# Expert results added into the residual stream in DRAM by accumulating scatters, in place of a gather by token at the end

## The chip, the cores and the metric

The kernel runs on one core of one Trainium2 chip. The time of a run is the device time of that core in microseconds (us). Three runs of the kernel before took 2021.2, 2023.53 and 2025.5 us; the median is 2023.53 us. A further execution was taken with the hardware profiler; its own time is 2023.36 us, and the span of its records, from the first to the last instruction, is 2021.5 us. Instants below are microseconds from the start of that span.

The engines are TensorE (PE: matrix products and transposes; PEld is its weight load), VectorE (DVE), ScalarE (ACT), GpSimd (POOL) and SyncE (SP). SP and ACT issue ordinary DMAs, and POOL issues the indirect ones, whose row numbers come from a tile of integers. Each engine takes its instructions in order, and waits at each for the semaphores that it names.

## What is computed

One decoder layer over 4 sequences of 1024 tokens, 256 wide, all in float32, in three blocks. The first is a gated delta rule with convolutions, the second a cross-attention over 77 context rows; each is followed by a layer norm. The third is a mixture of 8 experts, of which every token uses two:

```python
router_logits = xf @ router_w.T
probs = softmax(router_logits)
topv, topi = top_k(probs, 2)
probs = probs * mask                      # the two largest are kept
probs = probs / (probs.sum(-1) + 1e-9)
h = silu(xf @ gate_w[e] + gate_b[e]) * (xf @ up_w[e] + up_b[e])
expert_out[e] = h @ down_w[e] + down_b[e]
y = einsum('ne,ned->nd', probs, expert_out)
x = layernorm(x + y)
```

(The lines from `h` on stand for every expert `e`; the reference computes all eight and multiplies six by zero.) The result is the last `x`, 4 x 1024 x 256.

## The kernel before

The tokens are worked in 8 slabs. Slab `i` has 128 tokens of each of the 4 sequences, so a tile of 128 partitions x 4 x 256. The delta rule writes its layer-normed output to `xd`, a DRAM tensor with a row for each token. The cross-attention stage reads slabs back from `xd` into SBUF tiles `xs` (three buffers, `slab_in`), adds the attention's result and norms in place. It runs over 64 units (slab, sequence, half of the heads); the steps of one unit are interleaved with those of the next ones and with the routing of the slab finished last.

`route(i)` finds for each token of slab `i` its two experts. `sel[:, 0]` and `sel[:, 1]` are one-hot rows for the first and the second expert, `share` their two normed weights, `slots` the two row numbers at which the token's vector goes into `xg`, a DRAM tensor with a region of rows for each expert. POOL then scatters the slab's rows into `xg` (L1134): 8 indirect DMAs for each slab, 128 rows of 1 KB each. Slabs 0 to 4 are written back to `xd` (L1142) so that their buffers can take slabs 3 to 7; slabs 5 to 7 stay in SBUF.

Then the weights of all experts lie in SBUF (`wall`, `wdn`, and the biases `ball`), and a list of 71 tiles (NT) is made by `tiles()`: each tile is 128 consecutive rows of one expert in `xg`. `ei` and `ri` have the expert and the first row of each tile, as integers that engines load into registers. The rows behind the last token of an expert are zeros (L1258). Tiles that no expert needs point at a region of zeros.

The tile loop (L1330) runs five steps in a staggered order: in pass `j`, `fetch(j+3)`, `hidden(j)`, `turn_h(j-1)`, `turned(j+1)`, `down(j-2)`. `fetch` is a DMA of SP from `xg` into a tile `mx`. `turned` transposes it on PE, and ACT copies it out. `hidden` multiplies by the gate and up weights (L1292, 8 matmuls), adds the gate bias on DVE (`sge`, L1300), takes silu on ACT (L1301), adds the up bias on DVE (`pup`, L1302) and multiplies on DVE (`mh`, L1304). `turn_h` transposes that, `down` multiplies by the down weights (`pdn`, L1319), DVE adds the bias into `my` (L1327, three buffers), and SP writes `my` to row `j*128` on of `yg`, a DRAM tensor of tile results (L1328).

At the end `combine(i)` works slab after slab. For each of the 4 sequences and both experts POOL gathers 128 rows from `yg` by the token's row numbers `found` (L1345), DVE multiplies them by `share` and adds them to the slab (L1351). Then come the statistics of the layer norm on DVE (L1355, L1356), its root on ACT (L1359), two small operations on DVE (L1360, L1361), the normalisation on ACT (L1363, one activation for each sequence), and one DMA to the output (L1366).

The order of instructions on each engine is set when the kernel is built: a scheduler takes, on every engine, work of later steps ahead of work that it expects to be ready later. It also places the semaphore waits: a write to a tile's buffer waits until every reader of the tile that had the buffer before it is done, and for a DMA that is its landing.

Of the kernel before, what the change touches and what calls it, by code (L numbers as in the profile page):

```python
# [17 lines left out]
P = 128  # L18
# [25 lines left out]
NROW = NE * STRIDE + NE * P  # L44

EW = 2 * KC * FF
EV = FC * D
# [18 lines left out]
N_LT = N_ROWS + 2 * H * 4  # L66
N_FREE = N_LT + NE * NE
N_STEP = N_FREE + NE
# [4 lines left out]
def _consts():  # L73
    k = np.arange(P)[:, None]
    c = np.arange(P)[None, :]

    sq = np.zeros((NSQ, P, P), np.float32)
    sq[K_ID] = k == c
    sq[K_LE] = k <= c
    sq[K_GT] = k > c  # L80
    sq[K_NGE] = -1.0 * (c >= k)
    sq[K_ONE] = 1.0
    narrow = np.zeros((P, NNARROW), np.float32)
    narrow[:, N_POS : N_POS + SC] = np.arange(SC)
# [19 lines left out]
def kernel(ctx: ExitStack, tc: tile.TileContext, a: dict, out: bass.AP):  # L104
# [14 lines left out]
    def new_banks(name, bufs):  # L119
# [20 lines left out]

    xg = tc.dram_tile([NROW, D], F32, name="xg")
    yg = tc.dram_tile([NT * P, D], F32, name="yg")

# [5 lines left out]
    nc.sync.dma_start(out=bd, in_=br)  # L149
    zero = const.tile([P, 1, D], F32, name="zero")  # L150
    nc.gpsimd.memset(zero, 0.0)

    nc.scalar.dma_start(
        out=xg[NE * STRIDE :, :].rearrange("(p r) d -> p r d", p=P), in_=bc(zero, [P, NE, D])
    )
# [3 lines left out]

    xd = tc.dram_tile([NS * B * P, D], F32, name="xd")  # L160

# [628 lines left out]
    def slab_in(pool, i):  # L790
        xs = pool.tile([P, B, D], F32, tag="xs", name="xs", bufs=3)
        nc.sync.dma_start(out=xs, in_=tokens(i))
        return xs
# [140 lines left out]
    def queries(n):  # L934

        t = units[n]
        if t["half"] == 0:
            x = slabs[t["i"]][:, t["b"], :]
# [69 lines left out]
    def outputs(n):  # L1008
# [28 lines left out]
        if half == 1:  # L1037
            x = slabs[i][:, b, :]
            nc.vector.tensor_tensor(x, x, px[:, 0:D], ALU.add)
            layernorm(xp, x, x, "c")  # L1040

    slots, found = (ek.tile([P, NS, B, 2], I32, name=n) for n in ("slots", "found"))
    at = ek.tile([P, NS, B, 2], F32, name="at")
    share = ek.tile([P, NS, B, 2], F32, name="share")

# [6 lines left out]
    def route(i):  # L1052
# [60 lines left out]
        nc.vector.tensor_tensor(got, pair, bc(pw.unsqueeze(2), [P, B, 2, NE]), ALU.mult)  # L1113
        nc.vector.tensor_reduce(share[:, i], got, AX.X, ALU.add)
        nc.vector.tensor_reduce(red, share[:, i], AX.X, ALU.add)
        nc.vector.tensor_scalar_add(red, red, 1e-9)
        nc.vector.reciprocal(red, red)
        nc.vector.tensor_tensor(share[:, i], share[:, i], bc(red.unsqueeze(2), [P, B, 2]), ALU.mult)
        yield
# [8 lines left out]
        nc.vector.tensor_tensor(got, pair, bc(place.unsqueeze(2), [P, B, 2, NE]), ALU.mult)  # L1128
        nc.vector.tensor_reduce(at[:, i], got, AX.X, ALU.add)
        nc.vector.tensor_copy(slots[:, i], at[:, i])  # L1130
        for b in range(B):
            yield
            for k in range(2):
# [5 lines left out]
                )  # L1139
                apart(ins, "scatter")  # L1140
        if i + 3 < NS:
            nc.sync.dma_start(out=tokens(i), in_=xs)  # L1142
            slabs.append(slab_in(sp, i + 3))
# [52 lines left out]
    def tiles():  # L1196


        def t(name, shape, dt=F32):
# [21 lines left out]
        )  # L1221
        ex_, row = t("tex", [P, NT]), t("trow", [P, NT])
        nc.vector.tensor_reduce(ex_, past, AX.X, ALU.add)
# [9 lines left out]
        nc.vector.tensor_copy(ri, row)  # L1233

        n = NS * B * 2
        flat = at.rearrange("p i b k -> p (i b k)")
        gap = t("gap", [P, n, NE])
        behind = nw[:, N_FREE : N_FREE + NE]
        nc.vector.tensor_scalar(nt, nt, 1.0 * P, -1.0 * STRIDE, ALU.mult, ALU.add)
        nc.vector.scalar_tensor_tensor(  # L1240
            gap, bc(flat.unsqueeze(2), [P, n, NE]), -1.0 * STRIDE, bc(behind.unsqueeze(1), [P, n, NE]), ALU.add, ALU.is_gt
        )
        nc.vector.tensor_tensor(gap, gap, bc(nt.unsqueeze(1), [P, n, NE]), ALU.mult)
        moved = t("moved", [P, n])
        nc.vector.tensor_reduce(moved, gap, AX.X, ALU.add)
        nc.vector.tensor_tensor(flat, flat, moved, ALU.add)
        nc.vector.tensor_copy(found, at)
        return ei, ri

# [3 lines left out]
    for e in range(NE):  # L1253
# [4 lines left out]
        apart(nc.sync.dma_start(out=xg[bass.ds(row, P), :], in_=zero[:, 0, :]), "scatter")  # L1258
    ei, ri = tiles()
    r_scope.close()  # L1260
# [5 lines left out]
    def fetch(j):  # L1266
# [4 lines left out]
        )  # L1271
        t["x"] = ep.tile([P, D], F32, tag="mx", name="mx", bufs=4)
        nc.sync.dma_start(out=t["x"], in_=xg[bass.ds(t["row"], P), :])
# [40 lines left out]
    def down(j):  # L1314
# [3 lines left out]
        for f in range(FC):  # L1318
# [5 lines left out]
                stop=f == FC - 1,  # L1324
            )
        y = ep.tile([P, D], F32, tag="my", name="my", bufs=3)
        nc.vector.tensor_tensor(y, px[:, 0:D], ball[:, bass.ds(e * D + B_D, D)], ALU.add)  # L1327
        nc.sync.dma_start(out=yg[j * P : (j + 1) * P, :], in_=y)  # L1328

# [8 lines left out]
    def combine(i):  # L1338
        xs = slab_in(ep, i) if i + 3 < NS else slabs[i]
        mv = ep.tile([P, B, 2], F32, tag="mv", name="mv")  # L1340
        for b in range(B):
            x = xs[:, b, :]
            for k in range(2):
                g = ep.tile([P, D], F32, tag="part", name="part", bufs=8)
                nc.gpsimd.indirect_dma_start(  # L1345
                    out=g,
                    out_offset=None,
                    in_=yg,
                    in_offset=bass.IndirectOffsetOnAxis(ap=found[:, i, b, k : k + 1], axis=0),
                )  # L1350
                nc.vector.scalar_tensor_tensor(  # L1351
                    x, g, share[:, i, b, k : k + 1], x, ALU.mult, ALU.add
                )
            st = ep.tile([P, 6], F32, tag="st", name="st", bufs=4)
# [84 lines left out]
```

## Time and profile before

| | |
|---|---|
| median of three runs | 2023.53 us |
| the profiled execution, its own time | 2023.36 us |
| the profiled execution, its span | 2021.5 us |
| busy in the span | PE 1639.5, PEld 1166.7, DVE 1134.5, ACT 917.4, POOL 550.4 us |
| delta rule and preparation of attention | 0 to about 1000 |
| cross-attention and routing | about 1000 to 1478 |
| last loads of weights, first tiles | 1478 to 1530 |
| tile loop (from the first `my` to the last) | 1526.7 to 1926.4 |
| `combine` | 1926.4 to 2021.5 |
| gathers from `yg` in `combine` | 64, first at 1929.62, last at 2009.1 |

A "busy" time is that in which the engine executed; waiting, register work and the issue of DMAs by SP are not counted. The table of stages is read from the instants at which the groups of instructions begin and end. A DMA has two times in the profile: that of the issuing instruction, and the time from issue to landing, which is when the semaphore that tells of its end is set.

### The profile page before, as it was taken

The numbers are of one execution on the slowest core, as the hardware profiler recorded it, in microseconds if no ns is written. First come the engines' busy times: TensorE is split into PE (matmuls) and PEld (weight loads), VectorE is DVE, ScalarE is ACT, GpSimd is POOL, SyncE is SP. The second block draws the span as 40 slices with busy tenths as digits, with TensorE's granted clock in tenths as the row PEclk, the third lists the DMA queues.
The fourth block names the chain that finished last, engine by engine and source line by source line (L and its number), as shares of the span: only waits on it lengthen the run. The fifth ranks groups of instructions, "written<-read, shape, count | busy, mean of one in ns | idle before, by whom it ended". The sixth has DMA issues, their size and how long they took to land.

```text
span 2021.5 us, 28024 instructions
## 1 busy us (share of the span) xinstructions
PE 1639.5 (81%) x9524; PEld 1166.7 (58%) x9524; DVE 1134.5 (56%) x3199; ACT 917.4 (45%) x2161; POOL 550.4 (27%) x503
## 2 busy tenths in 40 slices
PE   4678888888898989969898889888839999999910
PEld 2356565657575757736676666666626666666600
DVE  4738575757585857344665656656534444444444
ACT  3435554546363645522766666666502222222212
POOL 2212222222212122141444555455510000000065
PEclk9879898989898989889999999999869999999955
DMA  3011111101010101030300110000062111111144
GB/s 111 17 32 22 32 22 31 24 22 32 17 34 20 30 16 46 16 105 20 147 22 32 41 34 32 22 32 21 22 242 73 47 46 46 45 48 45 35 141 137
DMA packets 118347, 98.97 MB, mean 49 GB/s; under 512 B 57803, under 2 KB 106303, under 8 KB 117951
## 3 DMA queue, kind: packets, MB, share of 16 engines
q1 hardware_dynamic: 108863, 77.24, 12.9%
q0 software_dynamic: 6144, 16.79, 2.6%
q10 hardware_dynamic: 3200, 3.16, 0.4%
q8 instruction: 78, 1.28, 0.3%
q14 instruction: 62, 0.51, 0.1%
HBM read 62.12 MB, written 35.03 MB: 48 GB/s over the span
## 4 chain that ended last, share of the span: by engine, by line
PE 51%; DVE 19%; ACT 11%; POOL 8%; issue 6%; DMA 5%; SPq 1%; POOLq 0%; ACTq 0%; DVEq 0%
PE pgt L1292 6%; PE pdn L1319 6%; PE pup L1292 6%; ACT sc L1001 4%; PE pp L257 3%; PE pxo L1029 3%; PE psc L984 2%; DMA part<-yg,found 2%; DVE v L269 2%; DVE kq L269 2%; PE pe L432 2%; POOL xg L1134 2%; PE pss L365 2%; DVE bp L455 2%; PE pq L949 2%
## 5 line engine op out<-in xcount | busy, mean ns | idle before, releaser
L1001 ACT ACTIVATE sc<-sc,ntop,rq 128x77 f32<-128x77 f32 x512 | 182.3, 445 | 56.3 <-DVE ntop L999 47.3
L1345 POOL DMA_INDIRECT part<-yg,found x64 | 61.2, 957 | 454.8 <-issue 442.6
L1029 PE MATMUL pxo<-vo,aT 128*128 128x256 f32 (+1 forms) x640 | 161.9, 392 | 0.0
L1301 ACT ACTIVATE sge<-sge 128x512 f32<-128x512 f32 x71 | 44.7, 630 | 253.6 <-DVE sge L1300 253.6
L257 PE MATMUL pp<-nT,wqkv 128*128 128x262 f32 x512 | 144.1, 415 | 0.0
L1292 PE MATMUL pgt<-wall,mxT 128*128 x284 | 135.6, 600 | 2.0 <-ACT mxT L1281 1.2
L1319 PE MATMUL pdn<-wdn,mhT 128*128 x568 | 134.2, 379 | 0.0
L1292 PE MATMUL pup<-wall,mxT 128*128 x284 | 133.9, 594 | 0.0
L1006 POOL TENSOR_TENSOR sc<-sc,den 128x616 f32<-128x616 f32 x64 | 77.9, 1217 | 182.8 <-DVE ntop L999 87.9
L984 PE MATMUL psc<-kbd,qT 128*128 128x154 f32 x512 | 88.7, 320 | 46.9 <-ACT qT L976 45.8
L1029 PEld LDWEIGHTS pxo<-vo,aT 128*128 128x128 f32 (+1 forms) x640 | 118.7, 196 | 13.8 <-ACT aT L1020 1.9
L949 PE MATMUL pq<-xwq,xT 128*128 128x512 f32 x256 | 121.7, 597 | 0.5 <-ACT xT L943 0.5
L984 PEld LDWEIGHTS psc<-kbd,qT 128*128 128x128 f32 x512 | 79.8, 207 | 68.4 <-ACT qT L976 51.5
L963 POOL TENSOR_TENSOR rq<-rq,nhalf 128x8 f32<-128x8 f32 x64 | 105.3, 1646 | 42.2 <-DVE rq L962 40.6
L269 DVE SCALAR_TENSOR_TENSOR kq<-pp,cols,kq 128x256 f32<-128x256 f32 x192 | 90.5, 478 | 46.3 <-ACT kq L267 44.3
L269 DVE SCALAR_TENSOR_TENSOR v<-pp,cols,v 128x256 f32<-128x256 f32 x192 | 91.3, 476 | 43.8 <-ACT v L267 42.0
L257 PEld LDWEIGHTS pp<-nT,wqkv 128*128 128x128 f32 x512 | 96.4, 201 | 32.8 <-issue 18.0
L1300 DVE TENSOR_TENSOR sge<-pgt,ball 128x512 f32<-128x512 f32 x71 | 49.1, 692 | 112.9 <-PE pgt L1292 112.9
L1319 PEld LDWEIGHTS pdn<-wdn,mhT 128*128 128x128 f32 x568 | 102.5, 190 | 11.0
L685 POOL TENSOR_TENSOR so<-so,nhalf 128x4 f32<-128x4 f32 x32 | 32.3, 1010 | 269.0 <-DVE so L684 269.0
L1020 ACT COPY aT<-pat 128x512 f32<-128x512 f32 (+1 forms) x128 | 54.7, 429 | 108.1 <-PE pat L1018 108.0
L1004 DVE TENSOR_REDUCE den<-sc 128x8 f32<-128x616 f32 x64 | 50.5, 789 | 80.7 <-ACT sc L1001 80.7
(285 smaller groups left out, 3693.1 us busy)
## 6 DMA issues: line engine op xcount, KB each, us to landing
mx<-xg SPq DMA_DIRECT2D x71, 128.0 KB, 2.0
yg<-my SPq DMA_DIRECT2D x71, 128.0 KB, 1.7
xs<-xd SPq DMA_DIRECT2D x13, 512.0 KB, 4.0
xi<-in_x SPq DMA_DIRECT2D x8, 512.0 KB, 4.1
am<-ab SPq DMA_DIRECT2D x16, 256.0 KB, 4.0
xd<-kd SPq DMA_DIRECT2D x32, 128.0 KB, 2.3
wall<-in_L_ffn_gate_w SPq DMA_DIRECT2D x8, 512.0 KB, 10.4
wall<-in_L_ffn_up_w SPq DMA_DIRECT2D x8, 512.0 KB, 10.8
```

The costliest lines, as they stand in the source:

```text
L257: mm(pp[:, 0 : 2 * (HALO + P)], lhsT=wqkv[:, kc, c * P : (c + 1) * P], rhs=nT[:, kc, 2 * j : 2 * j + 2, :].rearrange("p b t -> p (b t)"), ...
L269: nc.vector.scalar_tensor_tensor(ch, pre[:, :, n : n + P], cols[:, w0 + n : w0 + n + 1], ch, ALU.mult, ALU.add)
L949: mm(pq, lhsT=t["xT"][:, kc, :], rhs=xwq[:, kc, c0 : c0 + HH * XD], start=kc == 0, stop=kc == KC - 1,)
L963: nc.gpsimd.tensor_tensor(rq, rq, nhalf[:, :HH], ALU.pow)
L984: mm(ps[:, c * 2 * SC : (c + 1) * 2 * SC], lhsT=qT[:, 2 * g + c, :], rhs=kbd[:, half * XC // 2 + 2 * g + c, b, :], start=True, stop=True,)
L1001: nc.scalar.activation(sc[:, h], sc[:, h], AF.Exp, scale=rq[:, h : h + 1], bias=ntop[:, h : h + 1])
L1006: nc.gpsimd.tensor_tensor(sc, sc, bc(den.unsqueeze(2), [P, HH, SC]), ALU.mult)
L1020: nc.scalar.copy(aT[:w, c0:c1, :].rearrange("p c t -> p (c t)"), pt[:w, 0 : (c1 - c0) * P])
L1029: mm(px[:, 0:D], lhsT=aT[:w, c, :], rhs=vo[:w, b, half * NV + c, :], start=half == 0 and c == 0, stop=half == 1 and c == NV - 1,)
L1292: mm(ps, lhsT=t["xT"][:, c, :], rhs=wall[:, bass.ds(e * EW + off + c * FF, FF)], start=c == 0, stop=c == KC - 1,)
L1319: mm(px[:, 0:D], lhsT=t["hT"][:, f, :], rhs=wdn[:, bass.ds(e * EV + f * D, D)], start=f == 0, stop=f == FC - 1,)
L1345: nc.gpsimd.indirect_dma_start(out=g, out_offset=None, in_=yg, in_offset=bass.IndirectOffsetOnAxis(ap=found[:, i, b, k : k + 1], axis=0),)
```

## The change

Tile results are no longer stored in `yg` and gathered at the end. `xd` holds the residual stream of all 8 slabs, and each tile adds its rows to it by an indirect DMA that adds in DRAM (`compute_op=ALU.add`).

For that a tile has to know, for each of its rows, which token it is and what its share is. The rows of `xg` get 4 more numbers (`DX = D + 4`): the token's row in `xd`, the number of its first expert, and its two shares. `route` writes them into 4 more columns of the slab, so that the same scatter carries them. The zero rows carry the number of a spare row of `xd` instead (128 spare rows were added), one for each partition, and shares of zero. In `down`, DVE picks the share by comparing the first expert's number with the tile's (`mw`, three operations on one column), casts the row number to an integer (`mrow`), ACT multiplies `my` by the share, and POOL scatters. All slabs are now written to `xd`, also the last three. `tiles()` loses the calculation of `found`. `combine` loads the slab from `xd` and only norms it; its slab buffers are 4. The tile's `mx` gets 6 buffers in place of 4.

```diff
+DX = D + 4
-    xg = tc.dram_tile([NROW, D], F32, name="xg")
-    yg = tc.dram_tile([NT * P, D], F32, name="yg")
+    xg = tc.dram_tile([NROW, DX], F32, name="xg")
...
-    xd = tc.dram_tile([NS * B * P, D], F32, name="xd")
+    xd = tc.dram_tile([NS * B * P + P, D], F32, name="xd")
+    nc.scalar.dma_start(out=xd[NS * B * P :, :], in_=zero[:, 0, 0:D])
...
     def slab_in(pool, i):
-        xs = pool.tile([P, B, D], F32, tag="xs", name="xs", bufs=3)
-        nc.sync.dma_start(out=xs, in_=tokens(i))
+        xs = pool.tile([P, B, DX], F32, tag="xs", name="xs", bufs=3)
+        nc.sync.dma_start(out=xs[:, :, 0:D], in_=tokens(i))
         return xs
...
-        nc.vector.tensor_tensor(share[:, i], share[:, i], bc(red.unsqueeze(2), [P, B, 2]), ALU.mult)
+        nc.vector.tensor_tensor(xs[:, :, D + 2 :], share, bc(red.unsqueeze(2), [P, B, 2]), ALU.mult)
+        nc.vector.tensor_scalar(
+            xs[:, :, D], nw[:, N_STEP : N_STEP + B], nw[:, N_PART : N_PART + 1], float(i * B * P), ALU.add, ALU.add
+        )
+        first = rp.tile([P, B, NE], F32, tag="first", name="first")
+        number = nw[:, N_NUM : N_NUM + NE].unsqueeze(1)
+        nc.vector.tensor_tensor(first, sel[:, 0], bc(number, [P, B, NE]), ALU.mult)
+        nc.vector.tensor_reduce(xs[:, :, D + 1], first, AX.X, ALU.add)
...
+        nc.sync.dma_start(out=tokens(i), in_=xs[:, :, 0:D])
         if i + 3 < NS:
-            nc.sync.dma_start(out=tokens(i), in_=xs)
             slabs.append(slab_in(sp, i + 3))
...
-        t["x"] = ep.tile([P, D], F32, tag="mx", name="mx", bufs=4)
+        t["x"] = ep.tile([P, DX], F32, tag="mx", name="mx", bufs=6)
         nc.sync.dma_start(out=t["x"], in_=xg[bass.ds(t["row"], P), :])
...
+        e0, w = t["x"][:, D + 1 : D + 2], ep.tile([P, 2], F32, tag="mw", name="mw", bufs=4)
+        mine = ex_[:, j : j + 1]
+        nc.vector.scalar_tensor_tensor(
+            w[:, 0:1], e0, mine, t["x"][:, D + 2 : D + 3], ALU.is_equal, ALU.mult
+        )
+        nc.vector.scalar_tensor_tensor(
+            w[:, 1:2], e0, mine, t["x"][:, D + 3 : D + 4], ALU.not_equal, ALU.mult
+        )
+        nc.vector.tensor_tensor(w[:, 0:1], w[:, 0:1], w[:, 1:2], ALU.add)
+        row = ep.tile([P, 1], I32, tag="mrow", name="mrow", bufs=4)
+        nc.vector.tensor_copy(row, t["x"][:, D : D + 1])
         y = ep.tile([P, D], F32, tag="my", name="my", bufs=3)
         nc.vector.tensor_tensor(y, px[:, 0:D], ball[:, bass.ds(e * D + B_D, D)], ALU.add)
-        nc.sync.dma_start(out=yg[j * P : (j + 1) * P, :], in_=y)
+        nc.scalar.activation(y, y, AF.Identity, scale=w[:, 0:1])
+        nc.gpsimd.indirect_dma_start(
+            out=xd,
+            out_offset=bass.IndirectOffsetOnAxis(ap=row, axis=0),
+            in_=y,
+            in_offset=None,
+            compute_op=ALU.add,
+        )
...
     def combine(i):
-        xs = slab_in(ep, i) if i + 3 < NS else slabs[i]
+        xs = ep.tile([P, B, D], F32, tag="xs", name="xs", bufs=4)
+        nc.sync.dma_start(out=xs, in_=tokens(i))
         mv = ep.tile([P, B, 2], F32, tag="mv", name="mv")
         for b in range(B):
             x = xs[:, b, :]
-            for k in range(2):
-                g = ep.tile([P, D], F32, tag="part", name="part", bufs=8)
-                nc.gpsimd.indirect_dma_start(
-                    out=g,
-                    out_offset=None,
-                    in_=yg,
-                    in_offset=bass.IndirectOffsetOnAxis(ap=found[:, i, b, k : k + 1], axis=0),
-                )
-                nc.vector.scalar_tensor_tensor(
-                    x, g, share[:, i, b, k : k + 1], x, ALU.mult, ALU.add
-                )
```

More of the change, by code (lines that the diff above doesn't have):

```diff
@@ L66 @@
 N_LT = N_ROWS + 2 * H * 4
-N_FREE = N_LT + NE * NE
+N_NUM = N_LT + NE * NE
+N_FREE = N_NUM + NE
 N_STEP = N_FREE + NE
@@ L93, in _consts @@
     narrow[:, N_LT : N_LT + NE * NE] = (e[None, :] < e[:, None]).reshape(-1)
+    narrow[:, N_NUM : N_NUM + NE] = e
     narrow[:, N_FREE : N_FREE + NE] = e * STRIDE - 1
@@ L149 @@
     nc.sync.dma_start(out=bd, in_=br)
-    zero = const.tile([P, 1, D], F32, name="zero")
+    zero = const.tile([P, 1, DX], F32, name="zero")
     nc.gpsimd.memset(zero, 0.0)
+    nc.vector.tensor_scalar_add(zero[:, 0, D : D + 1], nw[:, N_PART : N_PART + 1], float(NS * B * P))
     nc.scalar.dma_start(
-        out=xg[NE * STRIDE :, :].rearrange("(p r) d -> p r d", p=P), in_=bc(zero, [P, NE, D])
+        out=xg[NE * STRIDE :, :].rearrange("(r p) d -> p r d", p=P), in_=bc(zero, [P, NE, DX])
     )
@@ L937, in queries @@
         if t["half"] == 0:
-            x = slabs[t["i"]][:, t["b"], :]
+            x = slabs[t["i"]][:, t["b"], 0:D]
             pt = bank("pxt", "pt")
@@ L1037, in outputs @@
         if half == 1:
-            x = slabs[i][:, b, :]
+            x = slabs[i][:, b, 0:D]
             nc.vector.tensor_tensor(x, x, px[:, 0:D], ALU.add)
             layernorm(xp, x, x, "c")
-    slots, found = (ek.tile([P, NS, B, 2], I32, name=n) for n in ("slots", "found"))
-    at = ek.tile([P, NS, B, 2], F32, name="at")
-    share = ek.tile([P, NS, B, 2], F32, name="share")
+    slots = ek.tile([P, NS, B, 2], I32, name="slots")
     free = ek.tile([P, NE], F32, name="free")
@@ L1113, in route @@
         nc.vector.tensor_tensor(got, pair, bc(pw.unsqueeze(2), [P, B, 2, NE]), ALU.mult)
-        nc.vector.tensor_reduce(share[:, i], got, AX.X, ALU.add)
-        nc.vector.tensor_reduce(red, share[:, i], AX.X, ALU.add)
+        share = rp.tile([P, B, 2], F32, tag="share", name="share")
+        nc.vector.tensor_reduce(share, got, AX.X, ALU.add)
+        nc.vector.tensor_reduce(red, share, AX.X, ALU.add)
         nc.vector.tensor_scalar_add(red, red, 1e-9)
         nc.vector.reciprocal(red, red)
-        nc.vector.tensor_tensor(share[:, i], share[:, i], bc(red.unsqueeze(2), [P, B, 2]), ALU.mult)
+        nc.vector.tensor_tensor(xs[:, :, D + 2 :], share, bc(red.unsqueeze(2), [P, B, 2]), ALU.mult)
[6 more added lines that the diff above has]
+        nc.vector.tensor_reduce(xs[:, :, D + 1], first, AX.X, ALU.add)
         yield
@@ L1128, in route @@
         nc.vector.tensor_tensor(got, pair, bc(place.unsqueeze(2), [P, B, 2, NE]), ALU.mult)
-        nc.vector.tensor_reduce(at[:, i], got, AX.X, ALU.add)
-        nc.vector.tensor_copy(slots[:, i], at[:, i])
+        at = rp.tile([P, B, 2], F32, tag="at", name="at")
+        nc.vector.tensor_reduce(at, got, AX.X, ALU.add)
+        nc.vector.tensor_copy(slots[:, i], at)
         for b in range(B):
@@ L1221, in tiles @@
         )
-        ex_, row = t("tex", [P, NT]), t("trow", [P, NT])
+        ex_, row = ek.tile([P, NT], F32, name="tex"), t("trow", [P, NT])
         nc.vector.tensor_reduce(ex_, past, AX.X, ALU.add)
@@ L1233, in tiles @@
         nc.vector.tensor_copy(ri, row)
[L1235 to L1239, printed above, removed]
-        nc.vector.scalar_tensor_tensor(
-            gap, bc(flat.unsqueeze(2), [P, n, NE]), -1.0 * STRIDE, bc(behind.unsqueeze(1), [P, n, NE]), ALU.add, ALU.is_gt
-        )
[L1243 to L1248, printed above, removed]
+        return ei, ri, ex_
     behind = ek.tile([P, NE], I32, name="behind")
@@ L1258 @@
         apart(nc.sync.dma_start(out=xg[bass.ds(row, P), :], in_=zero[:, 0, :]), "scatter")
-    ei, ri = tiles()
+    ei, ri, ex_ = tiles()
     r_scope.close()
@@ L1342, in combine @@
             x = xs[:, b, :]
-            for k in range(2):
-                g = ep.tile([P, D], F32, tag="part", name="part", bufs=8)
-                nc.gpsimd.indirect_dma_start(
-                    out=g,
-                    out_offset=None,
-                    in_=yg,
-                    in_offset=bass.IndirectOffsetOnAxis(ap=found[:, i, b, k : k + 1], axis=0),
-                )
-                nc.vector.scalar_tensor_tensor(
-                    x, g, share[:, i, b, k : k + 1], x, ALU.mult, ALU.add
-                )
             st = ep.tile([P, 6], F32, tag="st", name="st", bufs=4)
```

## The prediction

> **What bounds the kernel now.** I read the stages first, as the busy time of each engine in a stretch (columns: stretch and length; PE, PEld, DVE, ACT and POOL busy with counts; granted clock; DMA share; GB/s).
>
> ```profile
> 1530.00:1926.00 396.00, 395.91 (x1507) 249.60 (x1505) 170.28 (x273) 102.26 (x204) 0.00 (x0) 1.00 0.16 48
> 1926.00:2022.00 96.00, 0.00 (x0) 0.00 (x0) 44.73 (x145) 18.97 (x40) 61.22 (x64) 0.52 0.47 144
> ```
>
> The tile loop is bound by PE, 395.91 of 396 us at clock 1.00, with POOL empty. The end stage has no PE work at all: 64 gathers on POOL. Second, the DVE timeline of one tile of the loop, and of the end:
>
> ```profile
> 1840.83 0.42 DVE L1327 TENSOR_TENSOR my<-pdn,ball 128x256 f32<-128x256 f32 x1 [0.89 <-PE pdn L1319]
> 1842.55 0.69 DVE L1300 TENSOR_TENSOR sge<-pgt,ball 128x512 f32<-128x512 f32 x1 [1.29 <-PE pgt L1292]
> 1844.26 0.70 DVE L1302 TENSOR_TENSOR pup<-pup,ball 128x512 f32<-128x512 f32 x1 [1.02 <-PE pup L1292]
> 1845.07 0.69 DVE L1304 TENSOR_TENSOR mh<-pup,sge 128x512 f32<-128x512 f32 x1
> ...
> 1846.65 0.42 DVE L1327 TENSOR_TENSOR my<-pdn,ball 128x256 f32<-128x256 f32 x1 [0.89 <-PE pdn L1319]
> ```
>
> ```profile
> 1929.62 0.99 POOL L1345 DMA_INDIRECT part<-yg,found  x1 [435.61 <-issue]
> 1930.91 0.96 POOL L1345 DMA_INDIRECT part<-yg,found  x1 [0.30 <-issue]
> 1932.17 0.95 POOL L1345 DMA_INDIRECT part<-yg,found  x1 [0.30 <-issue]
> 1932.43 0.48 DVE L1351 SCALAR_TENSOR_TENSOR xs<-part,share,xs 128x256 f32<-128x256 f32 x1 [6.06 <-DMA part<-yg,found]
> ```
>
> A tile takes 5.82 us (1846.65 - 1840.83), and DVE waits for PE before three of its four operations: it has slack. At the end a gather starts every 1.25 us, and its data are there 2.81 us after its start. Third, the DMA view (median us from issue to landing):
>
> ```profile
> mx<-xg SPq DMA_DIRECT2D x71, 128.0 KB, 2.0
> xs<-xd SPq DMA_DIRECT2D x13, 512.0 KB, 4.0
> out<-xs SPq DMA_DIRECT2D x8, 512.0 KB, 3.5
> xd<-xs SPq DMA_DIRECT2D x5, 512.0 KB, 2.9
> xg<-xs,slots POOLq DMA_INDIRECT x64, 2.4
> part<-yg,found POOLq DMA_INDIRECT x64, 2.8
> ```
>
> **What goes: the gathers.** From the end of the last `my` (1925.95 + 0.42 = 1926.4) to the end of the span is 95.1 us. The new end, counted from the landing of the last scatter, with SP's queue as built (loads 0 to 3, outputs 0 and 1, load 4, outputs 2 and 3, loads 5 and 6, output 4, load 7, outputs 5 to 7; a load from the fifth on waits for the output four before it to land): load 0 lands at 4.0. A slab's statistics on DVE are (12.4 + 5.4)/8 = 2.2 us by the rows of L1355 and L1356, and the list takes two slabs before the first root, so 8.4. Root 0.30, reciprocal, L1361 and hops 1.0, four activations 2.07 (L1363 in the end stage), so output 0 issues at 11.7. Outputs 1 to 3 follow ACT and the next two slabs' statistics to 18.4; load 4 goes at 15.3 (output 0 landed, 3.5) and lands at 19.3; 2.2 + 1.0 + 2.07 later output 4 issues, and load 7 stands behind it: 25.1. It lands at 29.1, its slab is normed at 34.4, output 7 lands at 38. With 1 us to close: 39 us.
>
> **What is added beside other work.** For each tile three one-column operations on DVE (0.15 each by L171, 128x1) after `my`, inside the 1.29 us in which it waits for `pgt`; one ACT activation (0.59, as L1363), where ACT stands idle 3.59 us before L1301; one POOL instruction (about 0.95) on an empty POOL. SP loses 71 stores of 0.32 us; it had room. Fetches keep ahead, since the six `mx` buffers are freed when DVE and PE have read them, four tiles early. Without slack in the loop these would cost 71 x 0.5 on DVE; the next part says when they don't.
>
> **What is added on a path: a loop through the scatter.** In the changed kernel's instruction lists, the scheduler has moved `mw` and `mrow` of a tile up to where its `mx` has landed, four tiles early. DVE's queue per tile reads: `my` of tile s, `mw` of tile s+4, `sge`, `mrow` of tile s+4, `pup`, `mh`, `my` of tile s+1. `mrow` has 4 buffers, so `mrow` of s+4 waits for the scatter of tile s to land. That scatter was only just fed by the `my` a few instructions ahead. Behind `mrow` in DVE's queue stand `pup`, `mh` and the next `my`; PE waits for `mh`, ACT and POOL for `my`. So there is a loop: landing, hop 0.03, `mrow` 0.15, `pup` 0.80 to the start of `mh` (1844.26 to 1845.07), `mh` 0.70, `my` 0.42, hop 0.10, ACT 0.59, hop 0.30 (cast of `slots` ended 1483.20, POOL began 1483.49), and the scatter itself. Without it 3.09 us, say 3.07 since small operations overlap the next. With A the time from an accumulating scatter's start on POOL to its landing, a tile takes the larger of 5.82 and A + 3.07. The cover is gone above A = 2.75, and every microsecond more costs 67 (tiles 4 to 70 have such a wait).
>
> **A is the unknown.** Nothing in this trace adds in DRAM. From below: the plain scatter of as many rows, 2.4; an accumulating one does all of its work. Then the loop hides. From above: a gather and a scatter one after the other, 2.8 + 2.4 = 5.2; with the rows' descriptors written once (0.96 of POOL), 4.24. Rows follow each other, so reads and writes overlap in part; the middle of 2.4 and 5.2 is 3.8. I take 3.9: nearer to 4.24 than to the gather, since reading and writing DRAM are both in it.
>
> The Trainium skill, "DMA: Bandwidth & Descriptors", section "Anatomy of one DMA — SWDGE (gpsimd) path", fits a DMA as 2.0 us plus bytes over 436 GB/s; for 128 KB read twice that is an estimate of 2.6 us, the loop would hide, and the forecast would be 1977 us. The trace's gather alone is already above it, at 2.8. A rule there speaks against the change: "Rules for kernel authors" says to wait for the earlier DMA's semaphore wherever an accumulating DMA meets another access of the same bytes; the kernel does so, and by that rule alone (0.3 + A for each tile) the stage would bind only from A = 5.5.
>
> **The sum**, by the profiled execution. `my` of tile 67 begins at 1916.46; its scatter at +1.41 = 1917.87. The loop adds 67 x (3.9 + 3.07 - 5.82) = 77.1. The last four scatters land one after the other, their tiles being ready: 4 x 3.9 + 3 x 0.3 = 16.5. The end, 39. Two smaller things: before the first tile, loads run until 1501 and one more slab of 512 KB stands in that queue (2.9 us alone, DMA share 0.60 over the stretch): +2. In routing, three more DVE operations, 0.5 to 0.6 us (0.17 to 0.19 each by the rows of L1118 and L1082) for each of 8 slabs ahead of scatters that POOL's queue waits for: 0 to 5, taken as +2. Counted at nothing: rows of 1040 bytes in place of 1024 (before, SP waits 188 us for scatters in that stage in any case); the stores of slabs 5 and 6, which lie beside attention; the 6 operations that `tiles()` loses, 2.7 us on DVE before 1490.7, as the first tile waits for loads until 1501; and at the start the zeros for `xg`, which now wait for the constants to land and stand in ACT's queue ahead of three weight loads: the first needed of these was issued at 7.57, landed 5.7 later, and is first read at 22.40, so 9 us cover it. Total 1917.9 + 77.1 + 16.5 + 39 + 4 = 2054.5 of span, and 1.9 around it (2023.36 - 2021.5): 2056.4, to be held against 2023.36, which is 0.2 below the median of the runs. I say 2056. Each microsecond of A is worth 71 (67 + 4); the zero crossing is A = 3.43.
>
> **Rivals.**
> - *The addition is nearly free* (A up to 3.38): the end's gain stays. For it: the gather, which reads DRAM too, takes only 2.8. Against: it writes no DRAM. At A = 2.8 the time is 2056.4 - 1.1 x 71 = 1978; at 2.4, with the loop hidden, the last landing is 1926.4 + 0.99 + 2.4 = 1929.8, and the time 1929.8 + 39 + 4 + 1.9 = 1975. It decides below A = 3.43. Chance 0.28.
> - *It cancels*: A of 3.4 to 3.5, within 0.2% (4 us, what a measurement here can tell from no change). Chance 0.06.
> - *Rows of one DMA engine are added one behind the other.* 128 rows over 16 engines are 8 each; if each adds 0.4 us (the distance of gather and scatter, 2.8 - 2.4) to the first one's 2.8, A is 5.6, and the time 2177. For it: a packet that needs two reads. Against: plain transfers run their rows together. Chance 0.12.
> - *My forecast*: A of 3.5 to 5.2, the loop through the scatter takes PE's place, 2028 to 2149. Chance 0.54.
>
> **How the numbers follow.** Slower is 0.54 + 0.12 = 0.66, same 0.06, faster 0.28. The likeliest case's own range is 2028 to 2149; both signs hold much, so the range reaches over the cheap case, to its bound at A = 2.4 to 2.8, and up to A = 5.2: 1976 to 2149. About 0.04 lies below and 0.12 above.
>
> **What would show it.** Right: the new indirect DMA lands 3.5 to 5 us after its start; `my` to `my` is A + 3.1, near 7.0; DVE's idle time before `mrow` is released by the DMA into `xd`; PE falls from 395.91 of 396 to about 0.83 of the loop; no gathers, and about 39 us from the last landing to the end. Wrong: tiles still 5.82 apart with DVE waiting for PE, which means a small A; or an `mrow` that doesn't wait; or an end stage far from 39.

## The result and the profile after

The changed kernel takes 2042.4 us (median of seven runs, 2032.9 to 2047.1) against 2021.4 us for the kernel before in the same comparison (seven runs, 2018.9 to 2025.5). The ratio is 1.010, with a 95% interval of 1.0079 to 1.0121: the change costs 1%. The profiled execution of the changed kernel took 2041.6 us, its span is 2039.8 us; that of before is 2021.5.

The difference of the two spans, 18.3 us, has three parts, read from the first and the last `my` (1540.5 and 1990.8; before 1526.7 and 1926.0):

| | before | after | difference |
|---|---|---|---|
| start to the first `my` | 1526.7 | 1540.5 | +13.8 |
| first `my` to the last | 399.3 | 450.3 | +51.1 |
| last `my` to the end | 95.6 | 49.0 | -46.6 |

The stages of the changed kernel, in the columns of the first view of the prediction:

```profile
1530.00:1926.00 396.00, 365.78 (x1326) 214.58 (x1325) 180.35 (x474) 113.06 (x239) 90.28 (x59) 1.00 0.26 40
```

PE had been busy for 395.91 of these 396 us; now it has gaps, and 1326 matmuls fit in place of 1507 (the first 10 us of this stretch now lie ahead of the first `my`). One tile of the loop, from the timeline of DVE, ACT and POOL (start, duration, engine, line, operation; in brackets the idle time before it and what ended that):

```profile
1840.12 1.55 POOL L1340 DMA_INDIRECT xd<-my,mrow  x1 [5.01 <-ACT my L1339]
...
1843.89 0.15 DVE L1336 CAST mrow<-mx 128x1 int32<-128x1 f32 x1 [2.81 <-DMA xd<-my,mrow]
1844.02 0.70 DVE L1301 TENSOR_TENSOR pup<-pup,ball 128x512 f32<-128x512 f32 x1
1844.83 0.69 DVE L1303 TENSOR_TENSOR mh<-pup,sge 128x512 f32<-128x512 f32 x1
1845.43 0.41 DVE L1338 TENSOR_TENSOR my<-pdn,ball 128x256 f32<-128x256 f32 x1
...
1845.88 0.51 ACT L1339 ACTIVATE my<-my,mw 128x256 f32<-128x256 f32 x1 [3.33 <-DVE my L1338]
...
1846.67 1.55 POOL L1340 DMA_INDIRECT xd<-my,mrow  x1 [4.99 <-ACT my L1339]
```

This is a closed loop of 6.55 us (1846.67 - 1840.12). A scatter starts on POOL; 3.77 us later its landing lets DVE cast `mrow`, a column of 128 numbers for a tile four further on; behind that wait stand `pup`, `mh` and `my` of the next tile, and then ACT and POOL. `pup`, `mh` and `my` no longer wait for PE at all: where before each showed an idle time released by PE, or followed such a one, now they follow `mrow`. The group of `mrow` (from the costliest groups of the page: count, busy time, mean ns of one, idle time before them and what ended it) shows it for all tiles. In the chain of work that ended last (its shares of the span, by engine and line) the scatter into `xd` has the largest share:

```profile
L1336 DVE CAST mrow<-mx 128x1 int32<-128x1 f32 x71 | 10.9, 153 | 191.9 <-DMA xd<-my,mrow 191.9
```

```profile
DMA xd<-my,mrow 12%; DVE pup L1301 2%; ACT my L1339 2%; DVE my L1338 1%; DVE mh L1303 1%; DMA xs<-xd 1%; ACT xs L1371 0%; DVE st L1363 0%; DVE mrow L1336 0%; DVEq L1338 0%; DMA out<-xs 0%; DVEq L1303 0%; DVEq L1328 0%; DVE mv L1364 0%; DVE r L1368 0%
```

An operation of 0.15 us, done 71 times, has 191.9 us of waiting before it in all, and all of that is for the scatters. The DMA view (count, median us from issue to landing) has a first sign of what adding in DRAM costs: 3.8 us against 2.6 for the plain scatters into `xg` in the same kernel:

```profile
xd<-my,mrow POOLq DMA_INDIRECT x71, 3.8
...
xg<-xs,slots POOLq DMA_INDIRECT x64, 2.6
```

The end, from the timeline of POOL and SP: the last tiles' results are ready, and their scatters wait for one another; the loads of the slabs start when the last has landed.

```profile
1989.62 1.55 POOL L1340 DMA_INDIRECT xd<-my,mrow  x1 [2.98 <-DMA xd<-my,mrow]
...
1994.07 1.55 POOL L1340 DMA_INDIRECT xd<-my,mrow  x1 [2.90 <-DMA xd<-my,mrow]
...
1998.51 1.55 POOL L1340 DMA_INDIRECT xd<-my,mrow  x1 [2.89 <-DMA xd<-my,mrow]
...
2002.23 2.04 SPq L1358 DMA_DIRECT2D xs<-xd  x4
```

From 2002.23 to the end of the span are 37.5 us.

So the end is 46.6 us shorter without the gathers, as meant, the tile loop is 51.1 us longer, and 13.8 us come from a place ahead of the tiles. Two questions were put to the chip: is it this loop, and what in it; and where do the 13.8 us come from?

### The profile page after: what moved, and what is told of

Its sections match the earlier page's. It is cut to its first block, busy times and chain, and to the rows that moved or that the text cites. A ratio compares the mean times of both kernels' runs of the same rounds, so it can differ in the third digit from the quotient of the medians.

```text
span 2039.8 us, 28261 instructions
## 1 busy us (share of the span) xinstructions
PE 1674.2 (82%) x9524; PEld 1173.0 (58%) x9524; DVE 1144.2 (56%) x3438; ACT 945.2 (46%) x2232; POOL 598.7 (29%) x510
## 3 DMA queue, kind: packets, MB, share of 16 engines
q0 software_dynamic: 13296, 17.83, 5.3%
## 5 line engine op out<-in xcount | busy, mean ns | idle before, releaser
L1340 POOL DMA_INDIRECT xd<-my,mrow x71 | 110.3, 1554 | 385.2 <-ACT my L1339 376.4
L1035 PE MATMUL pxo<-vo,aT 128*128 128x256 f32 (+1 forms) x640 | 176.1, 418 | 0.0
L1291 PE MATMUL pgt<-wall,mxT 128*128 x284 | 142.2, 624 | 35.8 <-ACT mxT L1280 35.8
L1339 ACT ACTIVATE my<-my,mw 128x256 f32<-128x256 f32 x71 | 36.1, 509 | 230.4 <-DVE my L1338 229.3
L1035 PEld LDWEIGHTS pxo<-vo,aT 128*128 128x128 f32 (+1 forms) x640 | 128.1, 211 | 17.4 <-ACT aT L1026 1.9
L1336 DVE CAST mrow<-mx 128x1 int32<-128x1 f32 x71 | 10.9, 153 | 191.9 <-DMA xd<-my,mrow 191.9
L1291 PEld LDWEIGHTS pgt<-wall,mxT 128*128 128x128 f32 x284 | 48.9, 191 | 97.0 <-ACT mxT L1280 62.3
```

The lines of the kernel that those rows point to most:

```text
L1035: mm(px[:, 0:D], lhsT=aT[:w, c, :], rhs=vo[:w, b, half * NV + c, :], start=half == 0 and c == 0, stop=half == 1 and c == NV - 1,)
L1291: mm(ps, lhsT=t["xT"][:, c, :], rhs=wall[:, bass.ds(e * EW + off + c * FF, FF)], start=c == 0, stop=c == KC - 1,)
L1339: nc.scalar.activation(y, y, AF.Identity, scale=w[:, 0:1])
L1340: nc.gpsimd.indirect_dma_start(out=xd, out_offset=bass.IndirectOffsetOnAxis(ap=row, axis=0), in_=y, in_offset=None, compute_op=ALU.add,)
```

## Experiments on the tile loop

**More buffers, and still not enough.** The obvious cure for a wait on a buffer is more buffers.

```diff
-        e0, w = t["x"][:, D + 1 : D + 2], ep.tile([P, 2], F32, tag="mw", name="mw", bufs=4)
+        e0, w = t["x"][:, D + 1 : D + 2], ep.tile([P, 2], F32, tag="mw", name="mw", bufs=8)
-        row = ep.tile([P, 1], I32, tag="mrow", name="mrow", bufs=4)
+        row = ep.tile([P, 1], I32, tag="mrow", name="mrow", bufs=8)
```

> Theory (loop through the scatter): the time from tile to tile in the changed kernel, 6.55 us, is the landing of a scatter plus DVE, ACT and POOL behind it, since mrow of a later tile waits for that landing at DVE and pup, mh and the next my stand behind it. With 8 buffers the scheduler moves mrow 8 tiles ahead in place of 4, so that it waits for the very same landing, that of the scatter just fed: still 6.55 us a tile, 2042 us in all. Rival (too few buffers): with 8 of them a landing has four more tiles of time, no mrow waits, 5.82 us a tile, 67 x 0.73 = 49 us less, 1993 us.

Measured: 2037.0 us (one run). One tile of it:

```profile
1840.02 1.55 POOL L1340 DMA_INDIRECT xd<-my,mrow  x1 [4.93 <-ACT my L1339]
...
1843.82 0.15 DVE L1336 CAST mrow<-mx 128x1 int32<-128x1 f32 x1 [2.84 <-DMA xd<-my,mrow]
...
1846.60 1.55 POOL L1340 DMA_INDIRECT xd<-my,mrow  x1 [5.03 <-ACT my L1339]
```

The same wait and the same loop, 6.58 us. In the order of this profile each `mrow` stands 8 tiles ahead of its `my` in place of 4, and all casts but the first eight wait: the scheduler has used each further buffer to issue the cast one tile earlier, and it waits for the scatter that has just been fed, as before. The rival falls.

With 16 buffers of both (the same two lines, `bufs=16`) the buffer is no longer what limits how early the cast can go: a tile's row can be cast only once its `mx` is there, and there are six buffers of `mx`. In the profile the cast now stands nine tiles ahead of its `my`, far fewer than 16.

> Theory (loop through the scatter): a row of xg can be fetched at most 8 or 9 tiles ahead, since mx has 6 buffers that are freed by the transposes; with 16 buffers mrow therefore uses one whose scatter landed long ago and waits for nothing on DVE. The tile falls back to PE's 5.82 us, 67 x 0.73 = 49 us less than the changed kernel's 2042: 1993 us, DVE's idle time before mrow near 0 in place of 192 us, the scatter's landing still 3.8 us. Rival (the accumulating scatters themselves slow the loop, by their traffic or because POOL issues them one after the other): 6.55 us a tile stays, 2042 us.

Measured: 1990.4 us (four runs, 1983.4 to 1998.9), 0.985 of before (0.981 to 0.989), where 1993 was expected. From the timeline:

```profile
1842.13 0.42 DVE L1338 TENSOR_TENSOR my<-pdn,ball 128x256 f32<-128x256 f32 x1 [0.89 <-PE pdn L1318]
...
1842.73 0.14 DVE L1336 CAST mrow<-mx 128x1 int32<-128x1 f32 x1
...
1843.37 1.55 POOL L1340 DMA_INDIRECT xd<-my,mrow  x1 [4.26 <-ACT my L1339]
1843.85 0.69 DVE L1299 TENSOR_TENSOR sge<-pgt,ball 128x512 f32<-128x512 f32 x1 [0.84 <-PE pgt L1291]
...
1847.95 0.42 DVE L1338 TENSOR_TENSOR my<-pdn,ball 128x256 f32<-128x256 f32 x1 [0.89 <-PE pdn L1318]
```

`mrow` waits for nothing, DVE waits for PE again, and a tile takes 5.82 us (1847.95 - 1842.13). The scatters are as slow as ever, 3.7 us, and go out one for each tile as before, so it was neither their traffic nor POOL that made the loop slow. The time from the first `my` to the last is 399.3 us, that of the kernel before. The change with this edit beats the kernel before.

**What the addition costs.**

```diff
             in_=y,
             in_offset=None,
-            compute_op=ALU.add,
         )
```

> The scatter overwrites in place of adding, so the output is not the layer's. Theory (the addition prices the loop): the landing falls from 3.8 to the 2.4 to 2.8 us that plain scatters and gathers showed, POOL's issue from 1.55 to 0.96; the loop's sum is 2.78 + 2.6 = 5.4 us, below 5.82, so the tile is bound by PE at 5.82, and the last four scatters are 4 x 1.2 = 5 us shorter: 2042 - 49 - 5 = 1988 us. Rival (any indirect scatter of 128 rows that is waited for costs the same, adding is nearly free): landing 3.8, tile 6.55, 2042 us.

Measured: 1986.1 us (one run; 1988 was expected). A plain scatter of the same rows lands in 2.4 us, POOL is busy with it for 0.96 us in place of 1.55, and the tile is back at 5.82 with the buffers as they were:

```profile
xd<-my,mrow POOLq DMA_INDIRECT x71, 2.4
```

```profile
1843.62 0.42 DVE L1338 TENSOR_TENSOR my<-pdn,ball 128x256 f32<-128x256 f32 x1 [0.28 <-PE pdn L1318]
...
1847.28 0.15 DVE L1336 CAST mrow<-mx 128x1 int32<-128x1 f32 x1 [1.25 <-DMA xd<-my,mrow]
...
1849.44 0.42 DVE L1338 TENSOR_TENSOR my<-pdn,ball 128x256 f32<-128x256 f32 x1 [0.54 <-PE pdn L1318]
```

The loop is still there, for `mrow` still waits 1.25 us, but its sum, 2.4 + 2.78 = 5.2 us, is below PE's 5.82, and what ends last before `my` is PE. So the 1.4 us that the addition adds to a landing decide which of the two sets the pace.

**The same wait in another queue.**

```diff
-        nc.vector.tensor_copy(row, t["x"][:, D : D + 1])
+        nc.gpsimd.tensor_copy(row, t["x"][:, D : D + 1])
```

> The changed kernel with one word changed: the cast into mrow, still with 4 buffers, runs on POOL in place of DVE. It has to wait for the same landing, but what stands behind it on POOL is the next scatter, which waits for that landing anyway. Theory (it is the place of the wait, ahead of pup on DVE, that closes the loop): 5.82 us a tile, 2042 - 49 = 1993 us, though nothing about buffers or scatters is changed. Rival (the wait as such, wherever it stands, sets the pace): 6.5 us a tile or more, 2042 us.

Measured: 1994.7 us (one run; the kernel before took 2027.1 in one beside it).

```profile
1841.27 0.19 POOL L1336 CAST mrow<-mx 128x1 int32<-128x1 f32 x1 [2.32 <-DMA xd<-my,mrow]
1841.48 0.42 DVE L1338 TENSOR_TENSOR my<-pdn,ball 128x256 f32<-128x256 f32 x1 [0.89 <-PE pdn L1318]
...
1843.19 1.56 POOL L1340 DMA_INDIRECT xd<-my,mrow  x1 [1.74 <-ACT my L1339]
...
1847.07 0.18 POOL L1336 CAST mrow<-mx 128x1 int32<-128x1 f32 x1 [2.32 <-DMA xd<-my,mrow]
1847.30 0.42 DVE L1338 TENSOR_TENSOR my<-pdn,ball 128x256 f32<-128x256 f32 x1 [0.89 <-PE pdn L1318]
```

The cast waits for the landing as it did on DVE (2.32 us here, 2.81 there), with the same 4 buffers and the same scatter of 3.8 us. But what stands behind it on POOL is the next scatter, which has to wait for that landing in any case, and a tile takes 5.82 us (1847.30 - 1841.48). It is the place of the wait that cost 51 us, not the wait.

## Experiments on what comes before the tiles

From the first scatter of the first slab into `xg` to that of the last slab the changed kernel takes 442.3 us (1052.04 to 1494.37), the kernel before 429.8 (1053.70 to 1483.49). Before, the first scatters of one slab and the next are 64.9 to 65.1 us apart, but for the last (40.4); after, the first four distances are 68.1 to 68.2. In two experiments only the routing part of the change was put into the kernel before.

```diff
+DX = D + 4
...
+        nc.vector.tensor_scalar(
+            xs[:, :, D : D + 3], bc(nw[:, N_STEP : N_STEP + B].unsqueeze(2), [P, B, 3]),
+            nw[:, N_PART : N_PART + 1], float(i * B * P), ALU.add, ALU.add
+        )
+        first = rp.tile([P, B, NE], F32, tag="first", name="first")
+        number = nw[:, N_NUM : N_NUM + NE].unsqueeze(1)
+        nc.vector.tensor_tensor(first, sel[:, 0], bc(number, [P, B, NE]), ALU.mult)
+        nc.vector.tensor_reduce(xs[:, :, D + 3], first, AX.X, ALU.add)
```

> The kernel before with only the wider rows: xg of 260 columns, three more DVE operations for each slab in routing, scatters and fetches of 1040 bytes. In the changed kernel four slabs of attention took 68.1 us in place of 64.9, at a granted clock of 0.90 in place of 0.95. Theory A (the three operations and the wider rows shift the work so that the clock falls): the same here, four or more slabs at 68, 2021.4 + 10 to 13 = 2032 to 2034 us. Theory B (a matter of the execution, or of something else in the change): slabs at 64.9 to 65.5, 2021 to 2025 us.

Measured: 2037.7 us (four runs, 2035.4 to 2042.3), 1.0083 of before (1.0059 to 1.0107). Slabs are 68 us apart (1118.84, 1186.84, 1254.98, 1323.17, 1391.49), so the routing part alone loses 14 us, some 4 more than the upper figure expected: Theory A, as far as it goes. Then each of its two halves alone, first the operations without the wider rows, then the rows without the operations:

```diff
-DX = D + 4
+DX = D
...
+        more = rp.tile([P, B, 4], F32, tag="more", name="more")
         nc.vector.tensor_scalar(
-            xs[:, :, D : D + 3], bc(nw[:, N_STEP : N_STEP + B].unsqueeze(2), [P, B, 3]),
+            more[:, :, 0:3], bc(nw[:, N_STEP : N_STEP + B].unsqueeze(2), [P, B, 3]),
...
-        nc.vector.tensor_reduce(xs[:, :, D + 3], first, AX.X, ALU.add)
+        nc.vector.tensor_reduce(more[:, :, 3], first, AX.X, ALU.add)
```

> The kernel before with only the three more DVE operations of routing, whose results go to a tile that nothing reads; rows stay 1024 bytes. Theory A1 (the three operations move the work of attention so that the granted clock falls): four or more slabs of attention at 68 us, as in the kernel with operations and wider rows (2037.7 us against 2023.6). Theory A2 (the wider rows do it): slabs at 64.9, 2021 to 2025 us.

For the rows alone the three operations are left out, and POOL fills the columns:

```diff
         nc.sync.dma_start(out=xs[:, :, 0:D], in_=tokens(i))
+        nc.gpsimd.memset(xs[:, :, D:], 0.0)
         return xs
```

> The kernel before with only the wider rows (xg of 260 columns, scatters and fetches of 1040 bytes); the four columns are zeroed by POOL, one small operation for each slab. Theory A1 (the three DVE operations do it): slabs at 64.9, 2021 to 2025 us. Theory A2 (the wider rows do it): slabs at 68, 2032 to 2040 us.

Measured: 2024.6 and 2023.9 us (one run each), against 2021.9 for the kernel before in that comparison (2018.6 to 2025.3). Neither half costs what the whole does: with the operations alone slabs are 64.8 to 65.1 us apart, with the rows alone 64.3 to 64.9. Both theories fall, and what is left is something that only the two together have: the operations write into the slab buffer, which the scatters read. DVE's timeline of the kernel with the whole routing part shows it:

```profile
1200.22 0.41 DVE L185 TENSOR_SCALAR xs<-xs,mvc,rsc 128x256 f32<-128x256 f32 x1 [6.97 <-POOL rsc L176]
1201.32 0.23 DVE L1123 TENSOR_SCALAR xs<-nw 128x12 f32<-128x12 f32 x1 [0.69 <-DMA xg<-xs,slots]
1201.46 0.85 DVE L995 TENSOR_TENSOR sc<-psc,bias 128x308 f32<-128x308 f32 x2
```

and that of the kernel before, at the same place:

```profile
1197.02 0.41 DVE L181 TENSOR_SCALAR xs<-xs,mvc,rsc 128x256 f32<-128x256 f32 x1 [6.96 <-POOL rsc L172]
1197.35 0.86 DVE L991 TENSOR_TENSOR sc<-psc,bias 128x308 f32<-128x308 f32 x2
```

The row numbers need only constants, so the scheduler puts their operation (L1123; L1124 in the changed kernel) as early as a buffer allows. There are three slab buffers, and the profile has this operation three times at 870 to 872 us and then once behind the scatters of each of the slabs 0 to 4: there it writes into the buffer for the slab three further on, which eight scatters, just issued, still read. It waits 0.69 us for the last of them to land, and the attention's `sc`, which PE waits for, starts 1.24 us after the operation before it in place of 0.33. That is `mrow` over again. The cure is to make the operation depend on something late:

```diff
+    ids = ek.tile([P, NS * B], F32, name="ids")
+    nc.vector.tensor_scalar_add(ids, nw[:, N_STEP : N_STEP + NS * B], nw[:, N_PART : N_PART + 1])
...
-        nc.vector.tensor_scalar(
-            xs[:, :, D], nw[:, N_STEP : N_STEP + B], nw[:, N_PART : N_PART + 1], float(i * B * P), ALU.add, ALU.add
-        )
+        nc.vector.scalar_tensor_tensor(
+            xs[:, :, D], red, 0.0, ids[:, i * B : (i + 1) * B], ALU.mult, ALU.add
+        )
```

(`red` is times zero; it is there for the order alone.) On the kernel with the routing part:

> The kernel before with the wider rows and three operations (2037.7 us), but with the row numbers of a slab made from a table and from red, which routing has only just computed. In the kernels with both parts the scheduler had put that operation early, behind the norm of the slab before, where it waits on DVE for the landing of the scatters that still read the slab buffer (0.69 us of idle time before L1123 at 1201.32, released by the scatter into xg). Theory C (this wait, in a stretch where PE is short of work, delays the slab and draws the granted clock down): no such wait is possible here, slabs at 64.9 to 65.3, 2022 to 2026 us. Rival (rows and operations together, whatever the order): slabs at 68, 2034 to 2040 us.

and on the changed kernel with 16 buffers:

> The changed kernel with 16 buffers of mrow and mw (1990.4 us) and the same late row numbers. Theory C: attention gets its 64.9 us a slab back, 10 to 13 us less, 1978 to 1981 us. Rival: 1990 us.

Measured: 2033.8 us (one run) and 1976.2 us (four runs, 1973.1 to 1978.4). On the chip of this comparison the kernel before took 2031.5 us (11 runs, 2024.7 to 2045.0), so the first is within its runs, though 8 us above the expected figures, and its total decides nothing. Its profile does: the slabs are 64.4, 64.3, 64.8, 64.8, 64.8 and 64.8 us apart, and the first `my` is at 1529.3 in place of 1539.8 with the early operation. The time lies at the end, where the 64 gathers start from 1932.2 to 2020.6, over 88.4 us, against 79.5 in the profile of before. The second run was expected at 1978 to 1981; its slabs have the same distances, and its first `my` is at 1523.8 in place of 1539.6, 15.8 us earlier where 10 to 13 were expected. Theory C holds for the wait: the place of that one operation cost the routing part its time.

**How 0.9 us of delay came to cost 3.2 us.** The granted clock is the share of TensorE's full clock that the chip's throttle let through, 1.00 or 0.50 here. The stretches of one slab of the kernel before, and then of the changed kernel, cut about where it changes (the third column from the end; the stretch 1216.70 to 1223.90, at 1.00, is left out):

```profile
1183.64:1202.60 18.96, 13.74 (x71) 10.24 (x69) 8.76 (x21) 9.99 (x27) 13.37 (x13) 1.00 0.25 84
1202.60:1209.40 6.80, 4.37 (x17) 4.09 (x18) 4.40 (x9) 2.95 (x9) 3.68 (x3) 0.51 0.00 0
1209.40:1248.50 39.10, 37.08 (x200) 28.52 (x199) 26.74 (x84) 29.13 (x78) 15.99 (x14) 1.00 0.04 14
```

```profile
1188.24:1203.10 14.86, 11.47 (x60) 8.47 (x58) 6.04 (x15) 8.05 (x21) 11.38 (x11) 1.00 0.21 73
1203.10:1206.50 3.40, 3.12 (x8) 2.58 (x9) 2.98 (x8) 0.29 (x1) 0.39 (x1) 0.51 0.49 154
1206.50:1209.90 3.40, 0.62 (x4) 0.28 (x2) 0.80 (x1) 3.40 (x10) 2.44 (x2) 0.99 0.00 0
1209.90:1216.70 6.80, 6.17 (x21) 5.36 (x22) 4.69 (x12) 2.74 (x9) 3.40 (x3) 0.50 0.00 0
...
1223.90:1256.38 32.48, 30.56 (x161) 23.77 (x161) 22.64 (x72) 22.10 (x60) 13.48 (x12) 0.95 0.05 17
```

Where PE is short of work behind the slab's scatters, the clock is halved for 6.8 us before, and for 3.4 + 6.8 us after; the last row holds another 3.4 us of it, from 1240.56 (0.05 x 32.48 is 1.6 us lost, which at half speed is a stretch of 3.3). So the slab has 6.8 us more at half speed, which is 3.4 us of PE's work if it has work throughout, and it is 3.2 longer. The Trainium skill, "TensorE: Matmul & The Clock Gate", section "What's actually happening", says that the clock knows two states, half and full, and changes after windows of 3.4 us in which PE was idle or busy. The stretches of 3.4 and 6.8 us at 0.50 agree with that. The first two halvings of this slab nearly do: in the 3.4 us ahead of each, PE was busy for 0.9 us or less, though not idle throughout. The third, at 1240.56, does not: there PE had been busy for 2.66 of 3.41 us. The kernel before has such a stretch too (1230.06 to 1233.47, 2.67 us) with no halving behind it, so why the clock falls there is not shown.

Nor is the wait by itself enough. The changed kernel has it in five slabs, and four are longer. The fourth and the fifth, as whole slabs, and the wait in the fifth:

```profile
1256.40:1324.50 68.10, 59.23 (x285) 45.66 (x284) 40.55 (x115) 41.99 (x112) 33.04 (x28) 0.90 0.09 32
1324.50:1389.50 65.00, 56.13 (x286) 43.34 (x285) 40.34 (x115) 42.03 (x112) 33.09 (x29) 0.95 0.10 33
```

```profile
1338.97 0.23 DVE L1124 TENSOR_SCALAR xs<-nw 128x4 f32<-128x4 f32 x1 [0.63 <-DMA xg<-xs,slots]
```

The fifth waits for 0.63 us, the fourth for 0.66, but in the fifth the clock is halved for 6.8 us in all, as in the kernel before, and the slab takes 64.9 us from first scatter to first scatter. So the delay costs little of itself, and the 3.2 us come with the further stretches at half speed. That the delay sets these off is argued from the order of events; what decides when it does is not shown. The runs show that taking the wait away takes the 3.2 us away. Nor is it a plain count of such stretches: with the late row numbers the third slab has 10.2 us at half speed (a granted clock of 0.92) and takes 64.8 us. PE is busy for 6.2 of these 10.2 us, and for 12.6 of the 13.7 us at half speed in the slab of the changed kernel shown above.

## Experiments on the end, and the best version

```diff
-        xs = ep.tile([P, B, D], F32, tag="xs", name="xs", bufs=4)
+        xs = ep.tile([P, B, D], F32, tag="xs", name="xs", bufs=6)
...
-        nc.sync.dma_start(out=out[:, i * P : (i + 1) * P, :].rearrange("b p d -> p b d"), in_=xs)
+        nc.scalar.dma_start(out=out[:, i * P : (i + 1) * P, :].rearrange("b p d -> p b d"), in_=xs)
```

> The kernel with 16 buffers of mrow and mw (1990.4 us), with 6 buffers of xs in place of 4 in the last stage and its outputs issued by ACT in place of SP, so that no load stands behind an output in SP's queue. Theory (the order in SP's queue sets the last stage): the time from the last landing to the end falls from 37.5 us to what ACT can do, 4.0 for the first load, some 4.4 to its first output, seven slabs more at 2.8 (0.3 and 4 x 0.52 and an issue of 0.4), 3.5 for the last output and 1: 32 to 33 us, 1986 us in all. Rival (the bandwidth of 8 MB of loads and outputs sets it): no change, 37 us, 1990 us.

Measured: 1990.1 us (1987.8 to 1993.6), against 1990.4 (1983.4 to 1998.9) without the edit, in another comparison: the totals tell nothing. The profiles do: from the landing of the last scatter to the end of the span it is 34.3 us (1957.6 to 1991.9) in place of 37.3 (1949.6 to 1986.9). The gain is 3 us, not the 4.5 to 5.5 expected. Which of the two edits brings it, the buffers or the queue of the outputs, was not tried apart, and what holds the rest of the end is not shown.

All three edits together:

> All three edits on the changed kernel: 16 buffers of mrow and mw, late row numbers, and the last stage with 6 buffers of xs and outputs issued by ACT, which took it from 37.3 to 34.3 us. By theory C 1975 to 1978 us, some 45 less than before; by its rival 1987.

Measured: 1972.4 us (six runs, 1970.0 to 1975.7), 0.971 of before (0.969 to 0.974), on the chip on which before takes 2031.5; against the 2021 to 2024 us that it took in the other comparisons it is 2.4 to 2.5% less. That is 3 us below the expected figures. Its end is 34.1 us (1934.2 to 1968.3) where the kernel without the edit of the end has 37.9 (1933.4 to 1971.3), and 1976.2 us in all.

## Why the prediction was right, point by point

The forecast was 2056 us against 2042.4; the side and the loop that makes the kernel slower were right, and two terms were off in opposite directions. Against the profiled execution (2041.6) the sum of 2056.4 is 14.8 too high: 23.5 too much for the loop, 9.8 too little for what comes before the tiles, and 1.1 too much for the rest. Part of the closeness is this cancellation. Part is luck with A: nothing on record then measured it, and it was set at 3.9 between bounds of 2.4 and 5.2, not far above the 3.43 at which the sign turns. One reason given for it, 4.24 with the rows' descriptors written once, did not come out: the scatter that adds uses 144 packets where a plain one uses 48, and holds POOL for 1.55 us, not 0.96.

- **What goes: the gathers.** Right. From the last landing to the end 37.5 us, forecast 39.
- **The loop through the scatter.** Right in every link: the landing, `mrow` four tiles ahead on DVE, `pup`, `mh`, `my`, ACT, POOL, and PE's cover gone. A was taken as 3.9; the links shown give 3.77, the median is 3.8. The step that was mis-sized is the rest of the loop, 3.07: it is 2.78. From start to start `mh` to `my` takes 0.60 and not 0.70, for on DVE the next instruction starts before the one ahead of it has ended (1845.43, with `mh` running to 1845.52), where the prediction had added durations; `my` to ACT takes 0.45 and not 0.52, for the hop is 0.04 and not 0.10; ACT to POOL takes 0.79 and not 0.89, for this activation takes 0.51 and not 0.59. With landings of 3.6 to 4.1 a tile takes 6.62 us on average over the 67 (1540.45 to 1983.85), 0.80 above PE's, and the loop adds 53.6 where 77.1 stood.
- **The last four scatters, one after the other.** Right: 17.1 us from the start of the first to the landing of the last (1985.09 to 2002.2), forecast 16.5. Here too two terms cancel: the landings are 3.7 to 3.8 and not 3.9, and from a landing to the next start it is 0.73 and not 0.3.
- **Loads before the first tile, +2.** From the issue of `wdn` to that of the first `mx` 35.5 us in place of 32.5: +3.1.
- **Routing, +2, at most 5.** Wrong: 10.7 us (`wdn` is issued at 1483.47 in place of 1472.82). The step that failed is "three more DVE operations, 0.5 to 0.6 us". It priced the operations and what POOL waits for; it did not ask what one of them would itself wait for (the scatters that read its slab buffer, 0.63 to 0.82 us in five slabs), though the same pattern had just been found for `mrow`. Nor had it a term for the clock in a stage where PE is short of work.
- **Counted at nothing.** Rows of 1040 bytes: right, 2023.9 us with these alone. The rest (`mw`, POOL's issue, ACT's activation, fetches) is covered, as the kernel with 16 buffers shows, whose loop is as long as that of before. POOL's issue is 1.55 us and not 0.95, and still beside other work. Ahead of `sge` the first `mw` waits 0.58 us on DVE for ACT to scale the `my` just made, which was not foreseen; this lies beside the landing, ahead of DVE's wait of 2.81 us, and costs nothing.
- **The rivals.** *The addition is nearly free*, at A = 2.4, was put at 1975 us; the plain scatter, which has that A, took 1986. Most of the 11 us between them lies ahead of the tiles (its first `my` is at 1541.1, 14.4 late, where 4 had been put); the last scatters, one after the other, add 2.7, and the end is 1.6 shorter. *Rows of one DMA engine are added one behind the other*, at 5.6, does not occur. The Trainium skill's fit ("DMA: Bandwidth & Descriptors", section "Anatomy of one DMA — SWDGE (gpsimd) path") gave an estimate of 2.6 us for an accumulating scatter, and by it 1977 (with the prediction's own terms it is 1975): measured 3.8. For the plain one, 128 KB once, it gives an estimate of 2.3, and 2.4 was measured.
- **What would show it.** Landing 3.5 to 5, DVE's idle time before `mrow` released by the DMA, no gathers: all there. `my` to `my` is 6.6 and not 7.0. PE at 0.83 of the loop was too low a figure: its busy time is 0.92 (365.78 of 396), and by the count of matmuls it is 0.88 (1326 of 1507).

## What to carry to other kernels

When a change adds a small operation, ask what it waits for and what stands behind it in its queue, before asking how long it takes: here a cast of 0.15 us cost 51 us and a write of four numbers for each partition some 11, both because an early place in DVE's order made them wait for a transfer just begun. More buffers may only move such an operation further ahead; put it on the queue that has to wait for that transfer in any case, or tie it to a late input. And in a stage where PE is short of work, look at the granted clock: here a delay of under a microsecond cost 3.2 us in the four slabs in which further stretches at half speed came with it, and next to nothing in the fifth.

## What was not expected of the hardware

- A scatter of 128 rows of 1 KB that adds in DRAM lands 3.8 us after its start on POOL, a plain one 2.4. POOL is busy for 1.55 us in place of 0.96. It uses 144 packets in place of 48: the queue of indirect DMAs has 13296 packets with the addition and 6480 without, for 71 such scatters and 64 plain ones of 48 each.
- The granted clock goes from 1.00 to 0.50 and back in stretches of 3.4 us and multiples of it. In the kernel before it does so once in each of the first six slabs, for 6.8 us, every 64.9 us; in the changed kernel two or three times in each of the four long slabs.
- The kernel before takes 2021 to 2024 us in the median of three comparisons and 2031.5 on another chip. The one profile taken there of a kernel with gathers at its end has them start over 88.4 us in place of 79.5; whether the chip is the cause is not shown.
